# The Up stage of a two-layer adapter kernel: the product with B21 of two neighbouring pairs made of seven products of halves

## Chip, core and metric

The kernel runs on one core of a Trainium2 chip. The metric is device time in microseconds (us) of one execution; lower is better. Profile names: PE is TensorE, PEld its weight loads, DVE is VectorE, ACT is ScalarE, POOL is GpSimd, SP is SyncE, whose queue issues most DMAs.

## The reference

`x` is 128 samples of 128 x 1024 (f32). Each sample has a role of three (`itok`, negative values wrap). Two layers of the same form run one after the other, each with its own weights per role:

```python
h = gelu(x @ W_down[role] + b_down[role])          # 1024 -> 512, exact gelu
y = x + h @ W_up[role] + b_up[role]                # 512 -> 1024
out = (y - mean(y)) * rsqrt(var(y) + 1e-5) * gamma[role] + beta[role]
```

Everything is f32.

## The kernel before

**Order of samples.** The kernel computes, on the chip, a slot for each sample so that neighbours have one role where they can: the commonest role first, then octets of eight samples of one role (14 of them), and what is left as pairs and two single samples. A layer has two stages.

**Down stage.** Hidden values are made per octet, with two levels of the Winograd form (seven products in place of eight): 7 x 7 products of two 128 x 256 matmuls each (L730). They go to DRAM (`hq`, `hp`, `h1`).

**Up stage.** It walks over 65 items m = 0..64 (`SEQ`): 63 pairs of samples and two singles (m = 35, 36). A pair takes 7 units of the plan's time. Its hidden values `a` (two samples, four blocks of 128) are loaded into an `h` block by `Up.load`, its rows of x (or of the first layer's output) into an `x` block by `Up.load_rest`. POOL makes three sums of `a` (`winograd_sums`, L873 to L876; the second overwrites a21). PE then makes seven products, each of two 128 x 512 matmuls (L880): with B11, B21, T2, T1, T3, B22, T4, steps s1 to s7 in this order. The weights and their sums T lie in `wall`, three roles side by side (`wu`). A PSUM bank collects several products and DVE reads it in between: bank "b" is seeded with the bias by an ACT copy (`seeded`, L931) and takes B11, T2, T3, T4; bank "e" takes T1, B22; B21 has a bank of its own (`all_banks[6]`). After a product DVE adds the bank to a row half: `begin` (L988) where the half is not yet complete, `end` (L996) with a sum for the mean where it is.

**Normalization of a sample**, `finish`: `squares` is ACT's work on the mean (L1087, L1089), the squares (L1091) and the variance (L1092), then POOL's power -0.5 (L1093). `scaled` is DVE's multiplication with gamma (L1100; called gamma below). `stored` ends it: for sample 0 ACT multiplies (L1107) and POOL adds beta (L1108), for sample 1 DVE does both at once (L1110, the beta step). `away` stores the rows from SP (L1115 in layer 0, L306 in layer 1).

**What sets the order.** Every step is put on a list with a planned time (`at`), and the list is sorted; that fixes the order of the instructions of each engine. The engines then run in that order and wait for each other by semaphores. Steps of a pair are planned relative to its `base`: products at 0, 2, ... 12, seeds at -4 and 1.5, `squares` at 10.4 and 12.4, `scaled` 1.3 after them, `stored` 3.1 after them, loads at -11.5 and -7, sums at -5.5. Neighbouring pairs overlap by half: products of one alternate with those of the next.

In layer 0 the Up stage also prepares the second layer's weights: `DownHalf` and `UpHalf` load a part, make its sums T1 to T4 on DVE with ACT's copies (`Sums`, L384 and L379), inner sums on POOL (L361 to L364), and store them. From m = 21 on a pair may have another role than the one two before; its bias, gamma and beta are loaded under a flag (`load_table`, L502).

Of the kernel before, what the change touches and what calls it, by code (L numbers as in the profile page):

```python
# [10 lines left out]
F32 = mybir.dt.float32  # L11
# [9 lines left out]
P = 128  # L21
# [6 lines left out]
def kernel(  # L28
# [30 lines left out]
    def region(name, n):  # L59
        return const.tile([P, n], F32, name=name)  # L60
# [5 lines left out]
    results = region("results", 3 * 2048)  # L66
    NSTAGED = 5
    staged = region("staged", NSTAGED * 1024)

    hd = {}  # L70
    for g in range(NOCT):
# [4 lines left out]
    for s in range(2):  # L76
# [9 lines left out]
    ]  # L86
    up_scratch = [
        {t: dram.tile([R, P, 1024], F32, tag=f"u{layer}{t}", name=f"u{layer}{t}") for t in ORDER}
        for layer in range(2)
    ]  # L90
    bias_scratch = [dram.tile([R, H], F32, tag=f"bu{layer}", name=f"bu{layer}") for layer in range(2)]
# [384 lines left out]

    up_blocks = wall[:, 0 : R * 7168].rearrange("p (r n) -> p r n", r=R)

    def wu(name, place, j):
        at = ORDER.index(name) * 1024 + j * K  # L480
        if isinstance(place, int):
            return up_blocks[:, place, at : at + K]
        return up_blocks[:, ds(place, 1), at : at + K]

    def load_wu(layer, name, place):
        kw = {} if place == 0 else {"cond": reg(present, place, [ENG.SP], 1), "cond_hint": False}
# [103 lines left out]
        return t  # L590

    plain_blocks = {}

    class PlainItem:

# [17 lines left out]
        def prepare(self):  # L613
            self.bias = new_bias(self.layer, None if self.slots[0] < 2 else self.slots[0], self.tag)
            first = turn_of["results"] % 2
            k = (first, 1 - first, 2)[self.nth % 3]
            self.h = results[:, ts(k, 2048)][:, 0 : 4 * self.n].rearrange("p (f c) -> p f c", f=4)
            self.one = len(self.slots) == 1
            if self.one:
                self.bank = all_banks[(2, 0)[self.parity]]  # L620
                self.ps = [self.bank[:, ts(f, P)] for f in range(4)]
            else:
                self.ps = [all_banks[k] for k in ((6, 7, 1, 3), (2, 0, 4, 5))[self.parity]]

        def chunk(self, n):
            if self.one and n == 0:
# [32 lines left out]
    class Octet:  # L659
# [74 lines left out]
        def product(self, q, p):  # L734
            ps, d = self.ps.setdefault(q, {}), self.d[q]
            m = lambda ii, kk: self.m(q, ii, kk)
            if p == "p1":
                ps["b"] = bank("b")
            elif p == "p4":
                ps["e"] = bank("de")  # L740
            t, w, v = {
                "p1": ("b", "b11", lambda: m(0, 0)),
                "p2": ("x", "b21", lambda: m(0, 1)),
                "p3": ("b", "t2", lambda: d["d0"]),
                "p4": ("e", "t1", lambda: d["d3"]),
                "p5": ("b", "t3", lambda: d["d1"]),
                "p6": ("e", "b22", lambda: d["d2"]),
                "p7": ("b", "t4", lambda: m(1, 1)),
            }[p]
            self.multiply(ps[t], q, w, v(), p in ("p1", "p4"), True)  # L750
# [120 lines left out]
    def winograd_sums(dst, a, engine=nc.gpsimd):  # L871
# [3 lines left out]
        engine.tensor_tensor(dst[:, 0], a21, a11, sub)  # L875
        nc.gpsimd.tensor_tensor(dst[:, 2], a12, dst[:, 0], sub)  # L876

    def product(ps, a, w, place, start=False):
        for j in range(2):
            nc.tensor.matmul(  # L880
                ps, a[:, j], wu(w, place, j), start=start and j == 0, stop=j == 1, skip_group_check=True
            )

    before_last = []

    class Up:
# [20 lines left out]
                self.sums = both[:, 1024:1792].rearrange("p (m j c) -> p m j c", m=3, c=P)  # L907
            nc.sync.dma_start(hT, hd_of(self.slot))

        def load_rest(self):  # L910
            if self.ns == 1:
                self.x = staged[:, 2048 * (self.slot % 2) :][:, 0:1024].rearrange("p (s n) -> p s n", s=1)
            else:
                self.x = up_block("x", self.pair % 3).rearrange("p (s n) -> p s n", s=2)
            for s, src in enumerate(x_of(self.layer, self.slots, ENG.SP)):
                nc.sync.dma_start(self.x[:, s], src)

        def prepare(self):
            self.place = 0 if self.slot < 42 else reg(place_at, self.slot, [ENG.PE], R - 1)
# [6 lines left out]

        def seeded(self, t):
            ps = bank(t)
            if self.m < 4:
                cleared(ps)  # L930
            nc.scalar.copy(ps, self.t["bias"][:, ts("be".index(t), K)])  # L931
            self.ps[t] = ps

        def products(self):
            self.ps = ps = {}
            A = lambda i, k: self.a[:, i, ts(k, 2)]

            def s1():
                product(ps["b"], A(0, 0), "B11", self.place)
                self.begin(0, 0 if self.ns == 2 else 1, ps["b"])  # L940

            def s2():
                ps["a"] = all_banks[6]
                product(ps["a"], A(0, 1), "B21", self.place, True)
                self.end(0, 0, ps["a"])

            def s3():
                product(ps["b"], self.sums[:, 0], "T2", self.place)
                self.begin(0, 1, ps["b"])

            def s4():
                product(ps["e"], A(1, 0), "T1", self.place)
                self.begin(1, 1, ps["e"])

            def s5():
                product(ps["b"], self.sums[:, 1], "T3", self.place)
                self.end(1, 1, ps["b"])

            def s6():
                product(ps["e"], self.sums[:, 2], "B22", self.place)  # L960
                self.end(0, 1, ps["e"])

            def s7():
                product(ps["b"], A(1, 1), "T4", self.place)
                self.end(1, 0, ps["b"])

            def t2():
                product(ps["e"], A(0, 0), "T1", self.place)

            def t3():  # L970
                product(ps["b"], A(0, 1), "B21", self.place)
                self.end(0, 0, ps["b"])

            def t4():
                product(ps["e"], A(0, 1), "B22", self.place)
                self.end(0, 1, ps["e"])

            seeds = [({0: -3.4, 37: -2.9}.get(self.m, -4), lambda: self.seeded("b")), ({35: -1.65, 36: -0.65}.get(self.m, 1.5), lambda: self.seeded("e"))]
            if self.ns == 2:
                return list(zip(range(0, 14, 2), (s1, s2, s3, s4, s5, s6, s7))) + seeds  # L980
            return list(zip((0, 2, 4, 6), (s1, t2, t3, t4))) + seeds
# [16 lines left out]
        def finish_last(self):  # L998
# [28 lines left out]

            def begin_bank(item, s, cols, t):
                begun[item.m, cols.start] = ps = bank(t)
                nc.scalar.copy(ps, item.t["beta"][:, cols])  # L1030

            def by_tensor(item, y, name, cols):
# [40 lines left out]
        def finish(self):  # L1073
# [4 lines left out]
            for s in range(self.ns):  # L1078
# [38 lines left out]
                        i = reg(perm, slot, [ENG.SP], B - 1)  # L1117
                        result(i, box["o"], slice(0, H), nc.sync)

                steps += [(t, squares), (t + 1.3, scaled)]  # L1120
                if ending:
                    steps += [(t + (2.5, 4.65)[s], stored), (t + (3.6, 5.6)[s], away)]
                    continue
# [19 lines left out]
    for layer in range(2):  # L1143
# [122 lines left out]
        for m in range(NSEQ):  # L1266
            base = up_base[m]
            item = Up(layer, m)
            at(base - 11.5, item.load)
            at(base - 7, item.load_rest)  # L1270

            def go(item=item, base=base):
                item.prepare()
                for time, step in item.products() + item.finish():
                    at(base + time, step)

            at(base - 5.5, go)
            if m >= NSEQ - 4:
                at(base + 12.9, lambda p=item.pair: up_done("h", p % 4))
                if m >= NSEQ - 3:  # L1280
                    at(base + 17.2, lambda p=item.pair: up_done("x", p % 3))
            if m < 21:
                continue
            box = {}

            def known(box=box, m=m):
                box["r"] = reg(role_at, SEQ[m], [ENG.SP], R - 1)
                box["c"] = reg(two_changed, m, [ENG.SP], 1)

            prev2 = up_base[m - 2]  # L1290
            at(prev2 + 2.5, known)
            two_pair = SEQ[m - 2] < SLOT_ONE
            for which, time in (
                ("bias", 2.6),
                ("gamma", 14.6 if two_pair else 9),
                ("beta", (16.6 if m < NSEQ - 1 else 17.3) if two_pair else 11),
            ):
                at(
                    prev2 + time,
                    lambda box=box, which=which, layer=layer, m=m: load_table(layer, m % 2, which, box["r"], box["c"]),  # L1300
                )

        if layer == 0:
            for part in range(4):
                at(T - 5.8 + 2 * part, lambda part=part: load_raw(1, 0, top_role(ENG.SP), [nc.sync], parts=4, only=part))
            for n in range(4):
                job, start = DownHalf(1, 1 + n // 2, n % 2, staged), up_base[0] + 8 + 54 * n
                at(start, job.begin)
                for time, step in job.over_bank(start + 10, 2) + job.rest(start + 24, 2.5, 1.2, 8):
                    at(time, step)  # L1310
            for n in range(6):
                job, start = UpHalf(1, n // 2, n % 2, staged), up_base[0] + 272 + 25 * n
                at(start, job.begin)
                for time, step in job.over_bank(start + 8, 1.3) + job.rest(start + 17, 0.6):
                    at(time, step)
# [69 lines left out]
```

## Time and profile before

| | |
|---|---|
| median of 3 runs | 2997.32 us (2997.17 to 2997.52) |
| profiled execution | 2999.3 us, span 2997.3 us, granted clock 0.997 |
| Down stage, Up stage of layer 0 | to about 735 us, 735 to 1510 us |
| Down stage, Up stage of layer 1 | 1510 to about 2215 us, 2215 to 2997 us |
| busy in 2400 to 2500 us | PE 100, DVE 77, ACT 51, POOL 72 us |
| PE waits in the Up stage of layer 0 | 1.4 us in all |

Busy PE time is modelled and covers overlapping matmuls, so the pace is read from starts. A line of a timeline has the start, the length, engine, line of the code, operation, output and inputs, shape, count, and in brackets how long the engine was idle before and who ended that. An f32 matmul has two records of PE and two of PEld.

### The profile page before, as it was taken

What the parts mean: (1) busy time and instruction counts of PE and PEld (TensorE: products, weight loads), DVE (VectorE), ACT (ScalarE), POOL (GpSimd) and SP (SyncE); (2) the same over time, 40 slices, a digit from 0 to 9 for tenths busy, and PEclk for the clock granted to TensorE, in tenths of its full rate; (3) what the DMA queues carried; (4) which work ended last, traced back from release to release, by engine and by line L of the source; (5) the groups of instructions that cost most, each with busy time, mean ns of one, the idle gap of its engine ahead of it and who ended that gap; (6) DMA issues with size and microseconds to landing.
All of it is one profiled execution on the core that took longest, in us unless ns stands there. A gap on an engine that the chain in (4) does not pass through costs nothing. (4 is left out here: it accounts for less than half of the span.)

```text
span 2997.3 us, 43092 instructions
## 1 busy us (share of the span) xinstructions
PE 2973.5 (99%) x10292; PEld 1932.2 (64%) x10292; DVE 2317.0 (77%) x4230; ACT 1285.2 (43%) x2832; POOL 2200.3 (73%) x1965
## 2 busy tenths in 40 slices
PE   8999999999999999999999999999999999999999
PEld 6988888887444444444489888888864444444443
DVE  5488998885787787878865888888857777777777
ACT  1134433333555555555522333333335455554554
POOL 2399998886788887777714888888867777767775
PEclk8999999999999999999999999999999999999999
DMA  7788888455878887987797455675476666777664
GB/s 183 191 234 270 267 262 256 145 155 193 296 252 279 271 285 267 319 299 275 263 257 181 143 148 153 180 208 142 131 267 227 221 221 223 276 246 250 220 220 173
DMA packets 379888, 677.96 MB, mean 226 GB/s; under 512 B 39149, under 2 KB 263662, under 8 KB 379642
## 3 DMA queue, kind: packets, MB, share of 16 engines
q1 hardware_dynamic: 372770, 664.67, 70.1%
q0 software_dynamic: 3072, 8.39, 1.2%
q10 hardware_dynamic: 3800, 2.16, 0.3%
q8 instruction: 88, 1.44, 0.2%
q14 instruction: 158, 1.29, 0.1%
HBM read 676.63 MB, written 249.06 MB: 309 GB/s over the span
## 5 line engine op out<-in xcount | busy, mean ns | idle before, releaser
L1093 POOL TENSOR_TENSOR varu<-varu,mhalf 128x1 f32<-128x1 f32 x254 | 320.7, 1263 | 386.6 <-ACT varu L1092 383.1
L1100 DVE SCALAR_TENSOR_TENSOR units<-blocks,meanu,results 128x1024 f32<-128x1024 f32 x249 | 326.0, 1309 | 172.1 <-ACT units L1091 171.9
L579 DVE STREAM_TRANSPOSE blocks<-staged 128x512 f32<-128x512 f32 x400 | 274.8, 697 | 110.5 <-PE bank_x L630 43.5
L1087 ACT ACTIVATE partu<-statu 128x2 f32<-128x2 f32 x254 | 51.6, 203 | 682.5 <-DVE blocks L996 677.6
L880 PE MATMUL bank_s<-wall,blocks 128*128 (+1 forms) x704 | 331.0, 592 | 0.3 <-DVE blocks L988 0.3
L763 ACT ACTIVATE results<-results,bcolo 128x256 f32<-128x256 f32 x448 | 227.4, 508 | 207.5 <-DVE results L781 116.3
L880 PE MATMUL bank_u<-wall,blocks 128*128 (+1 forms) x672 | 315.9, 592 | 0.0
L1108 POOL TENSOR_TENSOR units<-units,results 128x1024 f32<-128x1024 f32 x125 | 301.7, 2414 | 3.5 <-ACT units L1107 3.5
L880 PE MATMUL bank_t<-wall,blocks 128*128 (+1 forms) x640 | 301.1, 593 | 1.2 <-ACT bank_t L931 1.1
L715 POOL TENSOR_TENSOR units<-blocks 128x512 f32<-128x512 f32 x196 | 250.5, 1278 | 67.6 <-DVE blocks L703 43.2
L1110 DVE SCALAR_TENSOR_TENSOR units<-units,varu,results 128x1024 f32<-128x1024 f32 x128 | 295.7, 2310 | 1.3 <-POOL varu L1093 1.3
L1091 ACT ACTIVATE units<-blocks,meanu 128x1024 f32<-128x1024 f32 x250 | 287.1, 1148 | 8.4
L724 POOL TENSOR_TENSOR units<-blocks,units 128x512 f32<-128x512 f32 x196 | 250.2, 1277 | 14.7 <-PE bank_w L730 3.6
L880 PEld LDWEIGHTS bank_s<-wall,blocks 128*128 128x128 f32 x704 | 133.6, 190 | 168.0 <-issue 158.2
L880 PE MATMUL bank_y<-wall,blocks 128*128 (+1 forms) x504 | 236.8, 592 | 0.0
L880 PEld LDWEIGHTS bank_u<-wall,blocks 128*128 128x128 f32 x672 | 127.5, 190 | 159.7 <-issue 149.9
L880 PEld LDWEIGHTS bank_t<-wall,blocks 128*128 128x128 f32 x640 | 121.2, 190 | 155.2 <-issue 143.1
L873 POOL TENSOR_TENSOR blocks<-blocks 128x256 f32<-128x256 f32 x126 | 191.9, 1523 | 26.8 <-DMA blocks<-hq 24.5
L730 PE MATMUL bank_y<-blocks,wall 128*128 128x256 f32 x784 | 201.2, 379 | 0.0
L880 PEld LDWEIGHTS bank_y<-wall,blocks 128*128 128x128 f32 x504 | 95.8, 190 | 119.1 <-issue 118.7
L880 PE MATMUL bank_x<-wall,blocks 128*128 (+1 forms) x352 | 165.4, 592 | 0.0
L329 POOL DMA_DIRECT2D wall<-in_L_cond_W_down_dram x224 | 38.7, 173 | 169.6 <-DMA wall<-in_L_cond_W_down_dram 120.8
(309 smaller groups left out, 6683.5 us busy)
## 6 DMA issues: line engine op xcount, KB each, us to landing
staged<-in_x_dram SPq DMA_DIRECT2D x512, 128.0 KB
mid<-units SPq DMA_DIRECT2D x128, 512.0 KB
staged<-mid SPq DMA_DIRECT2D x512, 128.0 KB
blocks<-in_x_dram SPq DMA_DIRECT2D x126, 512.0 KB
blocks<-mid SPq DMA_DIRECT2D x126, 512.0 KB
out_dram<-units SPq DMA_DIRECT2D x125, 512.0 KB
hq<-results SPq DMA_DIRECT2D x112, 512.0 KB
blocks<-hq SPq DMA_DIRECT2D x112, 512.0 KB
```

Source lines behind the costliest of these rows:

```text
L579: nc.vector.transpose(to[:, :, at_col : at_col + P].rearrange("p j (a t) -> p j a t", t=SQ), v[:, k])
L715: engine.tensor_tensor(d["d1"], m(0, 0), m(1, 0), sub)
L724: engine.tensor_tensor(d["d2"], m(0, 1), d["d0"], sub)
L730: nc.tensor.matmul(ps[:, 0:256], u, v[:, j], start=start and j == 0, stop=stop and j == 1, skip_group_check=True)
L763: nc.scalar.activation(y, y, AF.Gelu, bias=self.bias[:, f : f + 1])
L873: engine.tensor_tensor(dst[:, 1], a11, a21, sub)
L880: nc.tensor.matmul(ps, a[:, j], wu(w, place, j), start=start and j == 0, stop=j == 1, skip_group_check=True)
L1091: nc.scalar.activation(box["o"], self.x[:, s], AF.Square, bias=m, accum_out=v)
L1093: nc.gpsimd.tensor_tensor(v, v, mhalf[:, 0:1], ALU.pow)
L1100: nc.vector.scalar_tensor_tensor(box["o"], self.x[:, s], box["m"][:, 0:1], self.t["gamma"], add, mul)
L1108: nc.gpsimd.tensor_tensor(o, o, self.t["beta"], add)
L1110: nc.vector.scalar_tensor_tensor(o, o, v, self.t["beta"], mul, add)
```

## The change

Two neighbouring pairs of one role, m odd and m + 1, make their products with B21 together. The two blocks a(0,1) of both pairs (sample 0, hidden values 256 to 511) form a matrix of two by two blocks; B21 is cut into two by two blocks of 128 x 256; seven matmuls of 128 x 256 (`p1` to `p7`) replace four of 128 x 512. The groups are m = 5, 7, ... 27 and 39, 41, ... 63 of each layer.

- POOL makes four sums of the left blocks (`inner`, 128 x 128) into a new region `shared_d`, and once per role four sums of B21's blocks (128 x 256). The latter lie in the last 256 columns of the four `h` blocks (`tail`); those of the second and third role go to DRAM (`to_dram`) and come back under the role's flag (`reload`, four conditional loads per group from m = 21 on).
- `p1`, `p3`, `p5`, `p7` go into one bank, with DVE's reads in between; `p4`, `p6` into another; ACT copies p1's result (`carry`) to bank 6, where `p2` adds. DVE adds the results to the row halves in six adds of 256 columns (`flow`).
- The first pair now begins with T1 (s4) and its other products move: T1 0, B11 6, T2 8, B22 9.5, T3 10, T4 12. The second keeps B11 0, T2 2, T1 4, T3 8, B22 10, T4 12. B11's add becomes the one with the sum (`end`).
- Banks that were begun by half are cleared before their next full use (`whole`). The second pair's loads move to -13 and to -9 and -7 (sample 0, sample 1); gamma of the second pair moves to 2.3 and 1.5 after `squares`; the last `h` blocks of a layer are given back later, and the next layer's first banks are chosen by what the last pair left.

```diff
+    class Shared:
+        def of_weights(place, name, at):
+            b = lambda j, h: wu("B21", place, j, h, UNIT)
+            i0, i1 = {
+                "t1": lambda: (b(0, 1), b(0, 0)),
+                "t2": lambda: (b(1, 1), at["t1"]),
+                "t4": lambda: (b(1, 0), at["t2"]),
+                "t3": lambda: (b(1, 1), b(0, 1)),
+            }[name]()
+            nc.gpsimd.tensor_tensor(at[name], i0, i1, sub)
...
+        def reload(cls, layer, place, cond):
+            for u in range(4):
+                src = shared_scratch[layer][u][ds(place, 1)].rearrange("o p n -> p (o n)")
+                nc.sync.dma_start(cls.tail(u), src, cond=cond, cond_hint=False)
...
+        def m(self, i, k):
+            return (self.first, self.second)[i].a[:, 0, 2 + k]
+        def begin(self):
+            b, e = bank("e"), bank("b")
+            begun_in_part.extend((b, e))
+            self.ps = {"b": b[:, 0:UNIT], "x": all_banks[6][:, 0:UNIT], "e": e[:, 0:UNIT]}
...
+        def inner(self, name):
+            k, i0, i1, op = {
+                "d1": (1, lambda: m(0, 0), lambda: m(1, 0), sub),
+                "d3": (3, lambda: m(1, 0), lambda: m(1, 1), add),
+                "d0": (0, lambda: d[:, 3], lambda: m(0, 0), sub),
+                "d2": (2, lambda: m(0, 1), lambda: d[:, 0], sub),
+            }[name]
+            nc.gpsimd.tensor_tensor(d[:, k], i0(), i1(), op)
+        def product(self, p):
+            to, v, w = {
+                "p1": ("b", lambda: m(0, 0), lambda: b(0, 0)),
+                "p2": ("x", lambda: m(0, 1), lambda: b(1, 0)),
+                "p3": ("b", lambda: d[:, 0], lambda: t("t2")),
+                "p4": ("e", lambda: d[:, 3], lambda: t("t1")),
+                "p5": ("b", lambda: d[:, 1], lambda: t("t3")),
+                "p6": ("e", lambda: d[:, 2], lambda: b(1, 1)),
+                "p7": ("b", lambda: m(1, 1), lambda: t("t4")),
+            }[p]
+            nc.tensor.matmul(self.ps[to], v(), w(), start=p in ("p1", "p4"), stop=True, skip_group_check=True)
+        def carry(self):
+            nc.scalar.copy(self.ps["x"], self.ps["b"])
+        def flow(self, t, i, h):
+            y = (self.first, self.second)[i].x[:, 0, ts(h, UNIT)]
+            tt(y, self.ps[t], y, add)
+        def steps(self):
+            s = [(-1.9, self.begin), (2.3, self.carry)]
+            s += [(-2.4 + 0.1 * k, lambda n=n: self.inner(n)) for k, n in enumerate(("d3", "d0", "d1", "d2"))]
+            for p, t in dict(p1=2, p4=3.1, p3=4, p2=4.1, p5=5.3, p6=5.4, p7=6.5).items():
+                s.append((t, lambda p=p: self.product(p)))
+            for t, args in (
+                (3.2, ("e", 1, 1)), (4.3, ("b", 0, 1)), (4.4, ("x", 0, 0)),
+                (5.5, ("b", 1, 1)), (5.6, ("e", 0, 1)), (6.6, ("b", 1, 0)),
+            ):
+                s.append((t, lambda args=args: self.flow(*args)))
+    LATER = 39
+    SHARED = list(range(5, 29, 2)) + list(range(LATER, NSEQ, 2))
...
+            if self.m in SHARED:
+                seeds = [(2, lambda: self.seeded("b")), (-2, lambda: self.seeded("e"))]
+                return [(0, s4), (6, s1_end), (8, s3), (9.5, s6), (10, s5), (12, s7)] + seeds
...
+            if self.m - 1 in SHARED:
+                seeds[0] = (-1.7, seeds[0][1])
+                return list(zip((0, 2, 4, 8, 10, 12), (s1_end, s3, s4, s5, s6, s7))) + seeds
...
-                steps += [(t, squares), (t + 1.3, scaled)]
+                late = self.m - 1 in SHARED and self.m + 1 in SHARED
+                steps += [(t, squares), (t + ((2.3, 1.5)[s] if late else 1.3), scaled)]
...
-            at(base - 11.5, item.load)
-            at(base - 7, item.load_rest)
+            at(base - (13 if m - 1 in SHARED else 11.5), item.load)
+            if m - 1 in SHARED:
+                at(base - 9, lambda item=item: item.load_rest((0,)))
+                at(base - 7, lambda item=item: item.load_rest((1,)))
+                for time, step in Shared(before, item).steps():
+                    at(base - 7 + time, step)
+            else:
+                at(base - 7, item.load_rest)
...
-                at(base + 12.9, lambda p=item.pair: up_done("h", p % 4))
+                at(base + {NSEQ - 4: 21.5, NSEQ - 3: 14.5}.get(m, 12.9), lambda p=item.pair: up_done("h", p % 4))
```

## Prediction

> **What bounds the kernel now.** I read the page's shares first, then busy time by stretches, then the timeline of one pair in the Up stage of layer 1, engine by engine. The profiled execution took 2999.3 us around a span of 2997.3; the median of the runs is 2997.32, so the span serves as the base.
>
> ```profile
> PE 2973.5 (99%) x10292; PEld 1932.2 (64%) x10292; DVE 2317.0 (77%) x4230; ACT 1285.2 (43%) x2832; POOL 2200.3 (73%) x1965
> ```
> ```profile
> 2400.00:2500.00 100.00, 100.00 (x235) 44.27 (x234) 77.26 (x117) 50.98 (x110) 72.24 (x58) 1.00 0.66 219
> ```
> PE has no gap in the Up stage, and the clock is full. Fewer columns would shorten the span, as long as no other engine makes PE wait. The columns after the count are PEld, DVE, ACT, POOL, clock, DMA share, GB/s.
>
> ```profile
> 2409.75 1.88 PE L880 MATMUL bank_s<-wall,blocks 128*128 128x512 f32 x4
> 2411.47 1.88 PE L880 MATMUL bank_u<-wall,blocks 128*128 128x512 f32 x4
> 2413.18 1.88 PE L880 MATMUL bank_x<-wall,blocks 128*128 128x512 f32 x4
> 2414.90 1.88 PE L880 MATMUL bank_t<-wall,blocks 128*128 128x512 f32 x4
> ```
> ```profile
> 2010.29 1.03 PE L730 MATMUL bank_s<-blocks,wall 128*128 128x256 f32 x4
> ...
> 2018.92 1.03 PE L730 MATMUL bank_u<-units,wall 128*128 128x256 f32 x4
> ```
> Starts tell the pace. A product (two matmuls of 512 columns, four records) takes 1.717; so two pairs take 14 x 1.717 = 24.03. In the Down stage ten products of two 256-column matmuls take 8.63, so one matmul takes 0.4315. The small PEld loads (190 ns) already hide there.
>
> ```profile
> 2411.66 0.69 DVE L988 TENSOR_TENSOR blocks<-bank_s,blocks 128x512 f32<-128x512 f32 x1 [1.02 <-PE bank_s L880]
> 2412.52 1.28 DVE L1100 SCALAR_TENSOR_TENSOR units<-blocks,meanu,results 128x1024 f32<-128x1024 f32 x1 [0.16 <-ACT units L1091]
> 2413.72 0.68 DVE L996 SCALAR_TENSOR_TENSOR blocks<-bank_u,blocks 128x512 f32<-128x512 f32 x1
> ...
> 2416.29 1.28 DVE L1100 SCALAR_TENSOR_TENSOR units<-blocks,meanu,results 128x1024 f32<-128x1024 f32 x1 [0.50 <-ACT units L1091]
> 2417.49 0.68 DVE L988 TENSOR_TENSOR blocks<-bank_t,blocks 128x512 f32<-128x512 f32 x1
> 2418.53 0.69 DVE L996 SCALAR_TENSOR_TENSOR blocks<-bank_s,blocks 128x512 f32<-128x512 f32 x1 [0.36 <-PE bank_s L880]
> ...
> 2419.15 2.24 DVE L1110 SCALAR_TENSOR_TENSOR units<-units,varu,results 128x1024 f32<-128x1024 f32 x1
> 2421.31 0.68 DVE L996 SCALAR_TENSOR_TENSOR blocks<-bank_y,blocks 128x512 f32<-128x512 f32 x1
> ```
> ```profile
> 2414.45 0.20 ACT L1087 ACTIVATE partu<-statu 128x2 f32<-128x2 f32 x1 [1.63 <-DVE blocks L996]
> ```
> ```profile
> 2416.66 1.32 POOL L1093 TENSOR_TENSOR varu<-varu,mhalf 128x1 f32<-128x1 f32 x1 [2.45 <-ACT varu L1092]
> 2417.95 2.35 POOL L1108 TENSOR_TENSOR units<-units,results 128x1024 f32<-128x1024 f32 x1
> ```
> DVE is far from full but runs behind PE, in a fixed order. The last add of a sample (L996 at 2413.72) releases ACT 0.73 later (Q, 2414.45); gamma (L1100) starts at Q + 1.84; POOL's beta add (L1108) at Q + 3.50; DVE's own beta step (L1110) takes 1.21 of work but has to let L1108 end, so DVE's next instruction is at Q + 6.86. Before the change this lag is harmless: PE meanwhile makes products of other banks.
>
> **What is removed and added on PE.** Per group of two pairs four matmuls of 512 go (3.434) and seven of 256 come (3.02): 0.413 saved. The order has 50 groups (25 a layer): 20.7. It also has 12 more clears of a bank; one costs 0.216 (in the trace one starts at 738.82, the next product at 739.04): 2.6. PE alone: -18.1 us.
>
> **The new wait.** Let 0 be the start of the first pair's T1 product, which now comes first. PE's order is then, by start: T1 0.00, T3 of the pair before 1.72, p1 3.43, B22 of the pair before 3.87, p4 5.58, p3 6.01, p2 6.45, T4 of the pair before 6.88, p5 8.59, p6 9.03, B11 9.46, p7, B11 of the second pair, and so on: 23.62 in all. p5 adds to the bank that p3 left, so it must wait until DVE has added p3's result to its row. Between them lie only p2 and T4, 2.15 us. What does DVE do then? By the instruction order: add T1 of the pair before, gamma of the pair two before (sample 0), its last add (T4), gamma (sample 1), T1's add, T3's add, beta step L1110, B22's add, p4's add, p3's add. From the rows:
> - The T1 product of the pair before starts at -3.43 (T4 of the pair two before lies between). A DVE add that waits for PE starts 1.91 after its product (bank_s 2409.75, L988 2411.66): -1.52.
> - The add 0.60 (2417.49: in steady sequence the next may start 0.60 later), gamma 1.21 (2412.52 to 2413.72): the last add starts at 0.29.
> - Q = 0.29 + 0.73 = 1.02. L1110 is over at Q + 6.86 = 7.88.
> - B22's add 0.61, p4's add 0.34, p3's add 0.42 (256-column adds in the Down stage last 0.42 and step 0.34): 9.25. To PE 0.05, and about 0.10 of a weight load laid bare (at 2656.44 a copy of 0.58 ended, the load began 2657.07, and its product took 1.82 for 1.717): p5 starts at 9.40, not 8.59.
>
> So PE loses 0.80 a group (0.7 to 0.9, as the nine steps differ from pair to pair by a hundredth or two each) where it saves 0.413. Later needs then hold: T2 of the first pair waits for B11's add (done 12.9, wanted near 13.9), T2 of the second for its B11 add (15.0, wanted 15.8), the seed of B11's bank ends at 11.2 and is wanted at 12.2. Without the wait at p5 the second of these would be the next one late, by 0 to 0.4. The chain starts at a PE product, so the loss returns in every group: 24.42 against 24.03.
>
> **POOL.** Four sums of 128 columns are new. 256 columns last 0.73, 512 last 1.27, so an estimate for 128 is 0.46 each: 1.9 a group, POOL stays near 82%. Its place matters more: they begin at about -1.45, so one may be running when gamma starts at -0.92, and gamma then waits as L1110 waits for L1108. Bounds 0 to 0.46 a group; below nothing is excluded, as a sum only adds. Two steps of 0.53 put the second sum's start at -0.92 itself; I take 0.15, 7.5 us in all. The sums of weights (26 of 256 columns, 0.73) lie before POOL work with 3 us in hand: nothing, or 0.73 each if that is gone, 19.
>
> **DVE, layer 0.** Six adds come and two of 512 go: 6 x 0.34 - 2 x 0.60 = +0.84 a group, in the chain already. DVE also makes the next layer's weight sums (L384, 40 in this stage, 0.60 each). In the new order ten of them stand between the T1 add and p3's add, where nothing hides them: 6.0; bounds 0 and 40 x 0.60 = 24.
>
> The Trainium skill (VectorE: DVE Perf Modes, § TRN2 errata) speaks against cutting adds: a fixed cost per instruction, so tile by 512 or more; its PSUM formula makes 392 ns of 256 columns. Here the record lasts 413 ns but the next starts after 0.34; by the page's figure the wait would be some 0.05 longer, 2.5 us in all, and the row decides.
>
> **SP, DMA, ACT.** The second pair's input is loaded 1.5 units earlier, its rows in two parts: no bytes more. Four conditional loads of weight sums stand ahead of it from the pair 21 on; such skipped issues take 0.08 to 0.10 (L502), 0.4 a group, where the input has about 5 us before its POOL sums. The x rows wait for gamma (0.3), and DVE wants them at 8.5. If that cover is gone (DMA share 0.91 from 1200 to 1300 us), it costs 1 to 2 us in each of some six groups. ACT's copy of p1 stands after the scaling and a seed, done near 5.0, wanted 5.9. The later gamma of the second pair I set at nothing, since it moves behind three adds that p6 and p7 want and nobody waits for it but a later load of rows. The later return of blocks at the stage's end is also set at nothing: the blocks serve transposes of the next layer, which DVE makes there with 1 us and more of idle time between them (L579 waits 110 us in all); gone, it costs a few us once.
>
> Sum: 50 x (0.80 + 0.15 - 0.413) = 26.9, + 2.6 + 6.0 = 35.5; on 2997.3 that is 3032.8, say 3032. Own range: without collision and sums 50 x 0.387 + 2.6 = +22 (3019); with full collision +51 (3048).
>
> **Rivals.** (1) DVE is not late: if the beta step started ahead of POOL's L1108, DVE would be free 1.4 earlier and p5 would not wait. Then -18.1: 2979. It decides when the chain is 0.80 shorter; between, every 0.1 costs 5 us, and the second pair's T2 may take 0 to 0.4 of it: 2979 to 2991. For it: PE has no gap now, and DVE 23% idle. Against: L1108 starts 1.2 ahead of L1110 in the rows. Chance 0.20. (2) The loss just eats the saving, 0.24 to 0.48 a group: 50 x (0.24 - 0.413) + 2.6 = -6 to 50 x (0.48 - 0.413) + 2.6 = +6, 2991 to 3003, 0.06. (3) Input or rows land late as well, in layer 0: 3050 to 3070, 0.08. (4) The groups are not of one role, or fewer: the order shows 350 matmuls of 256 in the stage, so I give it nothing. The forecast has 0.66.
>
> **Numbers.** Two tenths of a per cent, 6 us, is what a measurement can tell. Faster 0.20, same 0.06, slower 0.74. The range goes from 2988, which takes in part of (1) and (2), to 3048.
>
> **What would show it.** Right: PE gaps of 0.7 to 1.1 before p5, released by DVE's add of p3, once per group, 24.3 to 24.7 between first T1 products; PE busy share in the Up stage near 96%; L1110 ending just before B22's add. Wrong: no gap there and groups of 23.6; or gaps released by ACT, POOL or a DMA.

## The result, and the profile after

The changed kernel takes 3091.65 us (median of 4 runs, 3081.11 to 3094.77) where the kernel before takes 2997.24: a ratio of 1.031 (95 % interval 1.029 to 1.032), 94 us slower. The direction was forecast, the size was not: 35 us were forecast, and the range ended at 3048. The ratios further down are to the kernel before in the same series of runs, where it took 2998 to 2999.

The lines of the code have moved: matmuls L880 are now L899, the seven products L981, POOL's inner sums L966, DVE's adds of them L988; begin and end are L1120 and L1128, gamma L1233, POOL's beta add L1241, the beta step L1243; loads of the input L1029, of rows L1037; stores of B21's weight sums L937, results L1248 and L311. POOL makes B21's weight sums at L923, the sums of a pair's input at L884 to L887 and the power at L1226. Below, "input" is the second pair's hidden values, and "rows" are x or, in layer 1, the first layer's output.

The shares of the whole span, from the page:

```profile
PE 2985.5 (97%) x10592; PEld 1990.6 (64%) x10604; DVE 2353.9 (76%) x4430; ACT 1294.7 (42%) x2882; POOL 2298.8 (74%) x2193
```

Three stretches by windows, two of layer 0 and a quiet one of layer 1 (columns after the first: PE, PEld, DVE, ACT, POOL, clock, DMA share, GB/s):

```profile
800.00:900.00 100.00, 88.81 (x224) 42.66 (x224) 75.25 (x121) 46.65 (x101) 80.99 (x81) 0.98 0.69 232
1200.00:1300.00 100.00, 90.48 (x222) 42.73 (x221) 71.04 (x116) 48.82 (x105) 66.33 (x62) 0.97 0.80 273
2900.00:3000.00 100.00, 96.88 (x253) 47.41 (x252) 76.23 (x131) 50.41 (x111) 80.82 (x74) 1.00 0.64 216
```

No engine is full, and layer 0 loses three times as much as the quiet stretch. The quiet stretch is the forecast's case. One group of it, from the timeline:

```profile
2836.14 2.69 DVE L1243 SCALAR_TENSOR_TENSOR units<-units,varu,results 128x1024 f32<-128x1024 f32 x1
...
2836.68 0.59 PE L981 MATMUL bank_x<-blocks,shared_d 128*128 128x256 f32 x2
...
2838.75 0.68 DVE L1128 SCALAR_TENSOR_TENSOR blocks<-bank_v,blocks 128x512 f32<-128x512 f32 x1
...
2839.36 0.41 DVE L988 TENSOR_TENSOR blocks<-bank_u,blocks 128x256 f32<-128x256 f32 x1
...
2839.69 0.41 DVE L988 TENSOR_TENSOR blocks<-bank_x,blocks 128x256 f32<-128x256 f32 x1
...
2840.20 0.67 PE L981 MATMUL bank_x<-blocks,shared_d 128*128 128x256 f32 x2 [0.78 <-POOL blocks L884]
```

p3 (2836.68) leaves its bank; DVE is in the beta step, then adds B22, p4 and p3 (bank_x at 2839.69, done 2840.10), and p5 starts 0.10 later, as the forecast has it. The bracket names POOL, but that L884 works on another pair's input. The add of the bank ended 0.10 before; e1 below decides between the two. Starts of p5 from group to group are 24.64 apart (2889.48, 2914.12, 2938.76).

Layer 0 and the first part of layer 1 show what the forecast lacks. One group of layer 1, of the timeline of SP, POOL, DVE and PE:

```profile
2352.52 2.39 POOL L923 TENSOR_TENSOR shared_d<-wall 128x256 f32<-128x256 f32 x2
...
2354.25 1.02 SPq L937 DMA_DIRECT2D s<-shared_d  x2
...
2356.05 0.80 SPq L1037 DMA_DIRECT2D blocks<-mid  x2
...
2356.95 0.52 SPq L1029 DMA_DIRECT2D blocks<-hq  x1
...
2364.13 0.45 POOL L966 TENSOR_TENSOR shared_d<-blocks 128x128 f32<-128x128 f32 x1 [5.61 <-DMA blocks<-hq]
...
2366.42 2.34 POOL L1241 TENSOR_TENSOR units<-units,results 128x1024 f32<-128x1024 f32 x1
2366.49 3.36 DVE L1243 SCALAR_TENSOR_TENSOR units<-units,varu,results 128x1024 f32<-128x1024 f32 x1 [1.90 <-POOL varu L1226]
...
2371.27 0.67 PE L981 MATMUL bank_w<-blocks,shared_d 128*128 128x256 f32 x2 [3.25 <-POOL blocks L885]
```

SP's issues stand in the order of the list. Its stores of B21's weight sums wait for POOL's L923, the first pair's rows follow, then the input. POOL's inner sums start 7.2 us after the issue of the input and have waited 5.61 for it; POOL's power and beta add stand behind the sums, DVE's beta step behind them, and p3's add behind that. The gap at p5 is 3.41 instead of 0.94. The waits of POOL over the whole span, and of DVE over layer 0's Up stage:

```profile
POOL shared_d L966 <- DMA blocks<-hq: 48.7, 16, 6.3
```
```profile
DVE blocks L988 <- DMA blocks<-in_x_dram: 14.8, 5, 4.5
```

(us in total, times, longest). Of POOL's 16 waits, six, 27 us in all, come where SP had stood 9.4 to 11.1 us before a store of B21's weight sums. To sum up a trace, I take the gaps between PE's starts in the Up stages beyond the paces of the prediction (1.717, 0.4315, 0.216). Not all of a gap so counted is waiting: behind some long waits the granted clock is 0.50 for 3.4 us or more, and the matmuls there start twice as far apart (last section). The third column has what that adds to the two before it:

| | gaps layer 0 | gaps layer 1 | of these at half clock | span less gaps |
|---|---|---|---|---|
| before | 2.7 | 1.4 | 0 | 2993.2 |
| after | 77.3 | 43.0 | 15.4 | 2972.9 |

PE's own work became 20 us shorter (forecast 18.1), and the gaps grew by 116 (up to 2.6 of it are 12 clears of banks that have no record in this trace). In the profiled runs of all versions below that have the change, span less gaps lies between 2970 and 2979: the gaps account for the loss.

### The profile page after: what moved, and what is told of

It is laid out like the page before. It is cut to its first block, busy times and chain, and to the rows that moved or that the text cites. A ratio compares the mean times of both kernels' runs of the same rounds, so it can differ in the third digit from the quotient of the medians.

```text
span 3093.1 us, 44659 instructions
## 1 busy us (share of the span) xinstructions
PE 2985.5 (97%) x10592; PEld 1990.6 (64%) x10604; DVE 2353.9 (76%) x4430; ACT 1294.7 (42%) x2882; POOL 2298.8 (74%) x2193
## 3 DMA queue, kind: packets, MB, share of 16 engines
q8 instruction: 91, 1.49, 0.2%
## 5 line engine op out<-in xcount | busy, mean ns | idle before, releaser
L1226 POOL TENSOR_TENSOR varu<-varu,mhalf 128x1 f32<-128x1 f32 x254 | 275.0, 1083 | 326.3 <-ACT varu L1225 319.2
L899 PE MATMUL bank_s<-wall,blocks 128*128 (+1 forms) x960 | 455.8, 597 | 4.3 <-DVE blocks L1128 4.1
L1233 DVE SCALAR_TENSOR_TENSOR units<-blocks,meanu,results 128x1024 f32<-128x1024 f32 x249 | 340.7, 1368 | 133.3 <-ACT units L1224 133.2
L899 PEld LDWEIGHTS bank_s<-wall,blocks 128*128 128x128 f32 x960 | 183.1, 191 | 206.5 <-issue 183.5
L1241 POOL TENSOR_TENSOR units<-units,results 128x1024 f32<-128x1024 f32 x125 | 301.1, 2409 | 10.1 <-ACT units L1240 10.1
L1243 DVE SCALAR_TENSOR_TENSOR units<-units,varu,results 128x1024 f32<-128x1024 f32 x128 | 282.0, 2203 | 18.2 <-POOL varu L1226 18.2
L899 PE MATMUL bank_t<-wall,blocks 128*128 (+1 forms) x544 | 256.9, 595 | 4.1 <-DVE blocks L1128 4.1
L899 PE MATMUL bank_u<-wall,blocks 128*128 128x512 f32 (+1 forms) x512 | 244.7, 601 | 0.5 <-DVE blocks L1128 0.5
L899 PE MATMUL bank_v<-wall,blocks 128*128 (+1 forms) x464 | 218.2, 592 | 0.1
L884 POOL TENSOR_TENSOR blocks<-blocks 128x256 f32<-128x256 f32 x126 | 185.7, 1474 | 22.4 <-DMA blocks<-hq 22.4
L899 PEld LDWEIGHTS bank_t<-wall,blocks 128*128 128x128 f32 x544 | 103.0, 190 | 112.6 <-issue 101.2
L899 PEld LDWEIGHTS bank_u<-wall,blocks 128*128 128x128 f32 x512 | 99.5, 194 | 114.6 <-issue 104.0
L741 PEld LDWEIGHTS bank_y<-blocks,wall 128*128 128x128 f32 x784 | 149.0, 190 | 20.2
L732 POOL TENSOR_TENSOR units<-units,blocks 128x512 f32<-128x512 f32 x84 | 107.0, 1274 | 61.0 <-PE bank_s L741 21.0
```

The source lines that it names most:

```text
L741: nc.tensor.matmul(ps[:, 0:256], u, v[:, j], start=start and j == 0, stop=stop and j == 1, skip_group_check=True)
L884: engine.tensor_tensor(dst[:, 1], a11, a21, sub)
L899: nc.tensor.matmul(ps, a[:, j], wu(w, place, j), start=start and j == 0, stop=j == 1, skip_group_check=True)
L1226: nc.gpsimd.tensor_tensor(v, v, mhalf[:, 0:1], ALU.pow)
L1233: nc.vector.scalar_tensor_tensor(box["o"], self.x[:, s], box["m"][:, 0:1], self.t["gamma"], add, mul)
L1241: nc.gpsimd.tensor_tensor(o, o, self.t["beta"], add)
```

## Experiments

Theories at the start. T1: the wait of the forecast, DVE's beta step standing ahead of p3's add. T2: the input is late by its place in SP's queue. Their rivals are that p5 waits for POOL, as its bracket says, and that the transfers themselves are late. A third, T3, came after the first three runs: rows are late as well.

**e1_beta_behind.** The second sample's beta step (and its store) behind the next group's adds:

```diff
-    steps.append((t + (3.2 if self.before_last else 3.1), stored))
-    steps.append((t + (5.4, 4.2)[s], away))
+    behind = s == 1 and self.m + 2 in SHARED
+    steps.append((t + (3.2 if self.before_last else 6.05 if behind else 3.1), stored))
+    steps.append((t + (5.4, 6.5 if behind else 4.2)[s], away))
-    ("beta", (16.6 if m < NSEQ - 1 else 17.3) if two_pair else 11),
+    ("beta", 18.6 if m in SHARED else (16.6 if m < NSEQ - 1 else 17.3) if two_pair else 11),
```

> Only the place of DVE's beta step of the second sample (with its store) changes in the pairs that make a group: it moves behind the next group's adds of p4 and p3. Theory T1 (DVE stands in the beta step while POOL makes the beta add, and p3's add is queued behind it): the quiet groups of layer 1 go from 24.64 to 23.6-24.0 us, the gap before p5 from 0.94 to under 0.4, and the stalls that a late beta add passes on shrink too; the time falls by 45 us or more, to 3045 or less. Rival R1 (p5 waits for its operand from POOL, as the trace attributes it): groups stay at 24.6, the time at 3085-3095.

3047.76 us (ratio 1.017, 1.015 to 1.019): 44 less, where 45 or more was expected. From the timeline of PE in layer 1:

```profile
2888.80 0.59 PE L981 MATMUL bank_x<-blocks,shared_d 128*128 128x256 f32 x2
...
2891.38 0.60 PE L981 MATMUL bank_x<-blocks,shared_d 128*128 128x256 f32 x2
...
2915.00 0.59 PE L981 MATMUL bank_x<-blocks,shared_d 128*128 128x256 f32 x2
```

The first line is p3, the others p5 of this group and the next. p5 follows p3 after 2.58 without a gap, and groups are 23.62 apart, the forecast's figure for PE alone. T1 holds, and the rival falls: nothing of POOL's operands was changed. POOL still waits for the input (58.8 us).

**e2_load_ahead.** The input ahead of the first pair's rows in SP's order:

```diff
-    at(base - (13 if m - 1 in SHARED else 11.5), item.load)
+    at(base - (14.05 if m - 1 in SHARED else 11.5), item.load)
```

> Only the place of the second pair's input load in SP's queue changes: ahead of the x loads of the first pair instead of behind them. Theory T2 (the input lands late because the load is queued behind loads that wait for DVE's gamma and behind stores that wait for POOL, and POOL's inner sums then wait 5 us): POOL's waits for DMA in the inner sums go from some 49 us in the two layers to under 15, the long gaps before p5 (2 to 6 us) go, the quiet groups stay at 24.64, and the time falls by about 50 us, to 3030-3050. Rival R2 (the transfers themselves or POOL's weight sums are late, not the place of the load): 3080-3095, long gaps stay.

3066.52 us (1.023, 1.022 to 1.025): 25 less, half of what was expected. The waits themselves went as T2 has it:

```profile
POOL shared_d L966 <- DMA blocks<-hq: 3.5, 5, 1.0
```

Gaps in layer 1 fell from 43.0 to 27.7, about the 25 times 1.02 of the quiet groups; in layer 0 they fell only from 77.3 to 64.2. Something else is late there.

**e3_both.** Both edits.

> Both moves together: the beta step behind the adds, and the load ahead of the x loads. If T1 and T2 both hold, quiet groups 23.6-24.0 and no long gaps: 2975-2995, at or below the kernel before. If only one holds, the time is that of the better single move, 3030-3050. If the two stalls hide each other, less than the sum of the two single gains.

3036.29 us (1.013, 1.011 to 1.015). The single gains, 44 and 25, do not add up: together they give 55. Part of the shortfall lies in PE's half clock: it adds 15.4 us in the changed kernel's trace, 5.8 in e1's, 7.5 in e2's and 11.3 in e3's, so either move alone takes 8 to 10 us of it away and both together 4. Layer 1 is nearly cured (gaps 10.1), layer 0 is not (52.4). DVE's waits in layer 0:

```profile
DVE blocks L988 <- DMA blocks<-in_x_dram: 29.6, 9, 5.1
```

Now p4's add, the first that touches the second pair's rows, stands waiting for them, with p3's add behind it.

**e5_half_more, e6_rows_early, e7_rows_alone.** Rows are loaded once a gamma has freed a block. A seventh half block should uncouple them; it had to be taken from the results (three slots instead of four). e6 also issues the rows earlier, e7 does this to the changed kernel without the two moves:

```diff
-    return ring("outs", 4, 1024, units)
+    return ring("outs", 3, 1024, units)
+    def x_half(m):           # rows: a ring of seven halves, in order of loading
+        k = x_turn[0] % 7
...
+        return units[:, 3072:4096] if k == 6 else up_block("x", k // 2)[:, ts(k % 2, 1024)]
-    at(base - 9, lambda item=item: item.load_rest((0,)))      # e6, e7
-    at(base - 7, lambda item=item: item.load_rest((1,)))
+    at(base - 13, lambda item=item: item.load_rest((0,)))
+    at(base - 9, lambda item=item: item.load_rest((1,)))
```

> The version with both moves, and the rows of x in a ring of seven halves of 1024 columns instead of three blocks of 2048 (the seventh half is taken from the ring of outputs, three slots instead of four). Rows are loaded at the same places in SP's order, but no longer wait for the gamma of the pair just before. Theory T3 (what is left, 57 us above the sum of PE alone, is DVE's add of p4 waiting for the second pair's rows, which are loaded only after a gamma and land 5 us later): DVE's waits for rows in layer 0 go from 29.6 us to 10-15, the time to 3010-3025. Rival (the rows are held by SP's queue, by its stores and weight loads, not by the gamma; or outputs become scarce): waits for rows stay near 30 us, the time at 3030-3045.

> As the seven halves, and the second pair's rows are issued 4 and 2 units earlier in SP's order, which the seventh half allows. T3: DVE's waits for rows in layer 0 under 5 us, stalls of PE there under 20 us (52 with both moves alone), groups of 23.6: 2980-3000, at or below the kernel before. Rival (layer 0's own extra work on DVE and SP, the sums and stores of the next layer's weights, makes the stalls): 3020-3040.

> The changed kernel with the seven halves and the early rows alone; the beta step and the input's load stay as the change has them. If the rows were the first thing late in the changed kernel: 3040-3060. If, as its trace reads (14.8 us of DVE's waits for rows in layer 0, and gaps at p5 that begin with the inner sums and with the beta step), they come after the two others: a gain of 5 to 20 us, 3070-3087, quiet groups 24.64 as before.

3069.70, 3071.22 and 3131.31 us: e5 and e6 33 to 35 above e3, e7 40 above the changed kernel. DVE's waits for rows in layer 0 fell from 29.6 to 19.6 at L988's place in e5, and e6's list has none of that add. But ACT now waits for a slot of a result, which its squares write first; e3 has no such wait. ACT's waits of e6 in layer 0 (L1243 is the squares here):

```profile
ACT units L1243 <- DMA mid<-units: 51.0, 19, 8.7
```

The rival "outputs become scarce" came true, so these runs do not say what timely rows are worth. They do say that three slots of results are too few here.

**e8_rows_on_act, e9_no_beta_move.** Only in layer 0, the rows of the second pair's first sample by ACT's queue instead of SP's, on e3 and on e2:

```diff
+    if layer == 0:
+        at(base - 8.55, lambda item=item: item.load_rest((0,), nc.scalar, ENG.Activation))
+    else:
         at(base - 9, lambda item=item: item.load_rest((0,)))
```

> The version with both moves; in layer 0 the rows of the second pair's first sample are loaded by ACT's queue, behind the scale of the sample before, instead of by SP's. Blocks and outputs are as in the kernel before. Theory T3' (those rows are held 4 to 7 us by what stands ahead of them in SP's order, stores of weight sums and of results, not by their gamma): DVE's waits for rows in layer 0 go from 29.6 us to under 8, PE's stalls there from 52 to under 30, the time from 3036 to 3000-3015; layer 1 stays. Rival (the transfer itself takes 5 us in layer 0, whichever queue issues it): waits near 25 us, 3030-3040. Second rival (ACT is held by the issue, its copies for p1 and the seeds come late): new gaps at the second matmul of p3 or at T2, no gain.

> The changed kernel with the input's load ahead and the rows on ACT's queue in layer 0; the beta step stays where the change has it. With input and rows in time, only the wait of the forecast is left: quiet groups 24.64, and 50 x (1.0 - 0.413) + 2.6 + 6 = 38 over the kernel before: 3030-3045. If rows were not held by SP's order: as with the input's load alone, 3060-3070.

3037.78 us (1.013, 1.012 to 1.015) and 3072.51 (1.024, 1.022 to 1.026): no gain (e9 is 6 above e2). On e8 DVE's waits for rows were spread, not removed (L988 25.4 us in 20 times, L1120 8.2). That the place of this one load in SP's order was the cause falls. Both figures are those of the first rival, the transfer's own time, which no run tests alone.

**e10 to e13: without the preparation.** Layer 0 differs from layer 1 by the preparation of the next layer's weights, so it was left out of e3, of the changed kernel, of the kernel before and of e2:

```diff
-    for n in range(4):
-        job, start = DownHalf(1, 1 + n // 2, n % 2, staged), up_base[0] + 8 + 54 * n
...
-    for n in range(6):
-        job, start = UpHalf(1, n // 2, n % 2, staged), up_base[0] + 272 + 25 * n
...
+    down_scratch[1], up_scratch[1] = down_scratch[0], up_scratch[0]
```

> The version with both moves, without the preparation of layer 1's weights in layer 0's Up stage (its loads, sums on DVE, ACT and POOL and stores are left out; layer 1 reads layer 0's weight sums for the second and third role, so its numbers are not the reference's, with the same transfers and products). Theory T4 (the 50 us of stalls that are left in layer 0 come from sharing DVE, POOL and SP with that preparation): PE's stalls in layer 0 fall from 52 us to 10-15, as in layer 1; 2985-3000. Rival (layer 0's own loads, x by a register's address, make the rows late): 3025-3040.

> The changed kernel as it is, without that preparation. T4: layer 0's stalls fall from 77 us to about the 43 of layer 1: 3050-3060. Rival: 3085-3095.

> The kernel before without that preparation: PE had no gaps beside it, so nothing should change: 2992-2998. If it does fall by more, that much of the other two results is the preparation's own and not the change's.

> The changed kernel with the input's load ahead and without the preparation: what the forecast's steps describe, but for its 6 us of sums. The wait at p5 alone, 0.94 to 1.0 in each of 50 groups less 0.413, and 2.6 for the clears: 24 to 30 over the kernel before, 3021-3030. If more is late than the input and the preparation's work: over 3040.

| | us | ratio to before | gaps layer 0, 1 | at half clock |
|---|---|---|---|---|
| e12 (before) | 2996.03, one run | | 0.2, 1.8 | 0 |
| e13 (input ahead) | 3029.30 | 1.011 (1.009 to 1.012) | 28.1, 26.4 | 0 |
| e11 (after) | 3060.95 | 1.021 (1.019 to 1.023) | 49.4, 41.5 | 10.1 |
| e10 (both moves) | 2994.00 | 0.9986 (0.998 to 0.9995) | 10.6, 10.4 | 0 |

T4 holds: with the preparation gone layer 0 loses nearly what layer 1 loses. To the kernel before the preparation costs 1 to 2.5 us (one run), to the changed one 31 (3091.65 - 3060.95), to e2 37, to e3 42. With the preparation left out of both kernels, e10 is 2 us below e12 (one run). POOL's waits for the input stay in e11, 59.0 us against 48.7, so they are not the preparation's. e13 is the forecast's own case, input and rows in time and no sums: 3029 lies in the 3021 to 3030 expected, and it has the quiet groups of 24.63. DVE's waits for rows in e10's layer 0, against 29.6 in e3 (the same add, one line lower):

```profile
DVE blocks L989 <- DMA blocks<-in_x_dram: 6.7, 4, 1.9
```

**e14_sums_only, e15_transfers_only.** Which part of the preparation costs the 42? e3 with the sums alone, and with the loads and stores alone:

```diff
     def store(self, name):            # e14, both classes
+        if self.layer == 1:
+            return
...
-    job.over_bank(start + 8, 1.3) + job.rest(start + 17, 0.6)
+    job.rest(start + 17, 0.6)          # e15, both jobs, and no inner sums
```

> The version with both moves, with the sums of layer 1's weights kept (on DVE, ACT and POOL, of what happens to stand in their buffer) and their loads and stores left out; layer 1 reads layer 0's weights. Theory T5 (of the 42 us that the preparation costs beside the change, the most is its transfers in SP's order and in the DMA engines): 2994-3008. Rival (the sums on DVE and POOL cost it): 3022-3036.

> The reverse: loads and stores of the preparation kept, its sums left out (the stores write what was loaded). T5: 3022-3036, DVE's waits for rows in layer 0 above 15 us. Rival: 2994-3008.

3009.87 us (1.0035, 1.002 to 1.005) and 3010.72 (1.0045, 1.003 to 1.006): 16 and 17 above e10. Neither is the most of it, so T5 and its rival both fall; together the two cost 42, more than their sum of 33. PE's half clock is part of the excess: it adds 11.3 us in e3's trace, 1.8 in e14's, 2.7 in e15's and none in e10's. DVE's waits for rows go with the transfers: 21.3 us at this add in e15's layer 0, 7.2 in e14's.

**e16_stores_later, e17_all_stores_later.** e3 complete, with SP's stores behind their sums, so that SP does not stand waiting with input and rows queued behind it:

```diff
-    at(up_base[m + 2 + 2 * n] + 6.8, lambda ...: Shared.to_dram(layer, place, names, kept))
+    for time, sums in ((6.8, True), (9.3, False)):          # the sums, then the stores
+        at(up_base[m + 2 + 2 * n] + time, lambda ...: Shared.to_dram(layer, place, names, kept, sums))
-    s.append((start + spread * n, lambda q=q, e=extra[:, n]: self.store(q, e)))     # e17
+    s.append((start + spread * n + (3 if self.layer else 0), lambda q=q, e=extra[:, n]: self.store(q, e)))
-    job.rest(start + 17, 0.6)                                                       # e17
+    job.rest(start + 20, 0.6)
```

> Correct again: the version with both moves, with the four stores of B21's weight sums per layer 2.5 units behind their sums in SP's order, where they waited 23 us in layer 0 for POOL with the input's load and the rows behind them. If that hold on SP is a good part of what is left: 3015-3028, and PE's gaps in the four groups shrink. If not: 3030-3040.

> The same, and the stores of layer 1's weight sums 3 units later too (SP waits for POOL and DVE there). If SP's waits for sums are what the preparation costs: 3000-3018. If it is the transfers' time in the DMA engines: as the one before, within 8 us.

3024.85 us (1.008, 1.007 to 1.010) and 3013.78 (1.005, 1.003 to 1.007): 11 less, and 11 less again. In e16 layer 1's gaps are down to 2.7, from 10.1, and layer 0's from 52.4 to about 49, so most of its 11 us come in layer 1; e17 leaves 33.1 in layer 0. SP's waits in layer 0 before the stores of B21's sums, in e3 and in e16 (one line lower):

```profile
SPq L937 <- POOL shared_d L923: 23.0, 8, 9.3
```
```profile
SPq L938 <- POOL shared_d L923: 4.5, 6, 1.3
```

So part of the loss is SP's order, and it can be had back by moving stores. e17 is the best version of the change that does all the work. It is 22.5 below e3 and still half a per cent slower than the kernel before; no version that does all the work was faster.

## Why the prediction was right in sign and wrong in size

In the order of its steps.

- **PE alone, -18.1.** Right: -20 by span less gaps, and 23.62 a group in e1.
- **The new wait, 0.80.** Right in mechanism and place: p5, behind p3's add, behind the beta step; e1 shows it by undoing it. p5's gap is 0.94 in the quiet groups, and the group 24.64, 1.02 above PE alone, where 0.95 was forecast with the collision of 0.15.
- **POOL's collision, 0.15.** It happens once in each quiet group from 2780 on: an inner sum takes 1.44 us instead of 0.46 beside a gamma, and that gamma 1.49 instead of 1.28. Its share of the 1.02 was not measured alone.
- **SP, DMA and the input, which have no term in the sum: this step failed.** The text gave the input "about 5 us before its POOL sums", and 1 to 2 us in some six groups if that cover was gone. The trace has 16 waits of 3 us on average and up to 6.3. Of what stands ahead of the input in SP's queue, the four conditional loads were priced, at their issue of 0.1; the waits of the stores of B21's weight sums were not. Without the preparation the input's place is worth 32 us (e11 less e13), with it 25 (after less e2). The half clock behind long waits is in these figures (10.1 in e11, none in e13) and had no term either.
- **Layer 0's sums, 6.0: mis-sized.** The preparation costs 31 beside the change as it is. Ten sums of 0.60 on DVE were counted, and its loads and stores in SP's queue were not: on e3 the transfers alone cost 17 (e15), the sums alone 16 (e14).
- **Later needs.** The forecast had a gamma release the rows' block at 0.3 and DVE want the rows at 8.5, so some 8 us for the load. p4's add, which takes the second pair's rows, waits 29.6 us for them in layer 0 once the two earlier waits are gone (e3).

In one chain of measured runs: 2997 before, 3029 with wait and PE alone (e13; the forecast's steps without sums and input give 3027), 3061 with the input in its place (e11), 3092 with the preparation (after). The forecast had +29.5, 0 and +6.0 for these; measured were +32, +32 and +31. The sign is no luck, as e13 has it from the forecast's own step. Rival (3), input or rows late in layer 0, named the right thing with 0.08 and priced it too low (3050 to 3070); nor is it layer 0 alone: e11 has 41.5 us of gaps in layer 1 against 26.4 in e13.

The Trainium skill bears on the failed step (DMA: Bandwidth & Descriptors, § Anatomy of one DMA — SWDGE (gpsimd) path): a DMA engine does not wait on semaphores, the wait is on the issuing sequencer before dispatch. What DMA engines do no run here shows; for SP the trace agrees, as it stands waiting before its issues. Its waits in layer 0's Up stage, after the change (735 to 1570 us) before loads of rows and stores of B21's sums, and before the change (735 to 1510 us) before loads of rows:

```profile
SPq L1037 <- DVE units L1233: 154.9, 66, 6.6
SPq L937 <- POOL shared_d L923: 30.4, 8, 11.1
```
```profile
SPq L916 <- DVE units L1100: 136.7, 69, 4.1
```

So SP's wait for gamma is hardly new. The waits before the stores are, with the input queued behind.

Open: what, beside the half clock, makes the preparation's sums and transfers cost 42 together where they cost 33 apart; what the last 33 us of e17 consist of (DVE still waits 14.0 for rows there); and what timely rows would be worth with four slots for results, which was not tried for want of SBUF.

## What to carry to other kernels

When a change makes a consumer need its data earlier, follow the load back through the queue that issues it: every instruction ahead of it counts with its wait, not with its issue time, and slack read from planned times is none. A stage that hides several side jobs at 100 % of PE hides them only as long as the engines' order has slack; once one engine runs just in time, each of them is paid for, here 31 us for what had cost 1 to 2.5. A long wait can cost more than its length, when the clock falls behind it. And a pace that is confirmed in a quiet stretch says nothing of the stretches where other work shares the queues: forecast each by its own rows.

## What was not expected of the hardware

- The bracket behind a wait can name the wrong engine. In the changed kernel 49 of the 50 p5 come more than 0.3 late; 38 of these brackets name POOL's L884 to L887 and 6 name DVE's L988, though DVE's add of the bank ended 0.10 to 0.15 before the matmul in all 49. e1 moved DVE's work alone, and the wait was gone in the quiet groups.
- Taking one slot of four from the results came with 33 us or more (e5 to e7) and with waits of ACT of up to 8.9 us (e7) for a store to land before the slot could be written.
- After some long waits PE runs at half its clock. p5 and p6 of one group of layer 0, behind a gap of 5.69; the windows are in that gap and behind it:

```profile
830.94 1.19 PE L981 MATMUL bank_w<-blocks,shared_d 128*128 128x256 f32 x2 [5.69 <-DVE blocks L988]
831.92 1.06 PE L981 MATMUL bank_t<-wall,shared_d 128*128 128x256 f32 x2
```
```profile
823.00:830.00 7.00, 2.25 (x7) 0.89 (x5) 2.49 (x3) 2.04 (x5) 4.37 (x6) 1.00 0.92 298
831.00:833.50 2.50, 2.50 (x5) 1.76 (x6) 1.63 (x6) 1.67 (x4) 0.74 (x1) 0.50 0.87 311
```

The granted clock is 0.50 there, and p6 starts 0.98 after p5 where 0.43 is the pace. The changed kernel has nine such stretches of 3.41 us in its Up stages, each 1.5 to 1.8 us longer for it. Not every wait brings one: behind 3.20 at 912.20 the clock fell, behind 3.25 at 2371.27 it did not. This loss lies in the gaps of the tables, so that span less gaps, 2973 both with it (after) and without it (e10), does not show it.
